# Transposing x by the DMA engine as 16-bit halves, with a new order of the first loads, in an attention and FP4 block on one core

## The chip, the cores and the metric

The kernel runs on one core of a Trainium2 chip. The core has five instruction engines that run side by side and meet at semaphores: TensorE (PE, with its weight loads listed as PEld), VectorE (DVE), ScalarE (ACT), GpSimd (POOL) and SyncE (SP), which here only issues DMAs. Sixteen DMA engines move the data. The metric is the device time of one execution in microseconds (us); lower is better.

## The reference, cut to what matters

The input is x of 16 batches, each 512 rows of 256 numbers in float32. All arithmetic is float32 unless said otherwise.

```
q, k, v = x Wq + bq, x Wk + bk, x Wv + bv          # 16 heads of 16 numbers
q, k    = softmax over the 16 numbers of a head     # p / (sum p + 1e-6)
ctx     = (q k^T / (sum q + 1e-6)) v                # linear attention: q (k^T v)
x1      = layernorm(x + ctx Wo + bo)
fp4(t)  = blocks of 16 along the last axis, rounded to a 4-bit grid, times the block's scale
g, u    = fp4(x1) fp4(w_gate)^T, fp4(x1) fp4(w_up)^T        # 704 numbers each
out     = layernorm(x1 + fp4(silu(g) * u) fp4(w_down)^T)
```

## The kernel before, in words

Work is cut into batches (16, called b) and into pairs (32, called i): a pair is 256 rows, two row tiles of 128, so a batch holds two pairs. The first half of the kernel, the attention, goes by batches; the second, the feed-forward part, goes by pairs.

For one batch, `load_x` brings the 512 rows into a tile `x` by a DMA that SP issues. `project` handles one pair. It calls `transposed` (line 617), which has TensorE turn four blocks of 128 by 128 of x into PSUM by multiplying with an identity matrix; ScalarE copies the result to `xT` (line 620). TensorE then multiplies `xT` by the weights of q and k (line 724, 512 columns at a time) and of v (line 734, 256 columns). A float32 multiplication is two instructions in the profile, a transpose is one. VectorE adds the biases as it empties the banks (lines 727 and 740) and finds the largest value of each head (line 746), GpSimd subtracts it (line 750). `features` takes the exponential on ScalarE for a whole batch (line 761), sums it on VectorE (763 to 774) and scales it on GpSimd (line 780). `key_values` forms k^T v and multiplies it with Wo (lines 793 and 807). `attend` transposes q on TensorE (again `transposed`), multiplies (line 835) and calls `norm`. GpSimd has prepared x plus the bias of Wo as `xb` (line 828), and that is the last use of the tile `x`. The finished x1 goes to DRAM from ACT's DMA queue and comes back later (line 853) into one of `X1` buffers.

`norm` is a layer norm in five steps on three engines: VectorE adds and sums (line 678), ScalarE forms the negative mean and the squares (685, 687), GpSimd takes the reciprocal root with a power (691 to 693), ScalarE writes the result (700). For the very last pair it is called once for each of its two row tiles.

For one pair, `quantise` rounds x1 to FP4 codes, which a DMA transposes as 16-bit numbers from SBUF to SBUF (line 864, tile `xcT`); the scales are transposed by TensorE, written to DRAM and read back spread out (line 666), and GpSimd multiplies both (line 869). `gate_up` is 64 matmul instructions of 352 columns (line 889), a SiLU on ScalarE (894), a product on VectorE (896), and the rounding of the result in `codes` (lines 635 to 648). The codes go through a transposing DMA of 128 by 1408 (line 928, tile `hcT`). `down` multiplies with w_down (line 946), adds x1 in `norm` and writes the output. The weights are themselves rounded to FP4 inside the kernel, by `weight_scales` and `fp4_exact`, a long run of VectorE, GpSimd and ScalarE instructions (lines 477 to 548), before the first `gate_up` can start.

The order of all this is not that of the source. Every step is recorded in a `Plan` with an engine, a cost in us, a due time, and what it reads and writes. `Plan.order` simulates the engines and, among the steps that can start, takes the earliest and at a tie the one with the least due time. The result is a fixed order on each engine; at run time each engine follows its own order and waits at semaphores. Each tag of a tile has a fixed number of buffers, and a step that needs a new one waits until the oldest is free. Eight banks of PSUM are used: seven are shared by the transposes, the gate and up products and all other products. `LEAD = 9` sets the due times of attention so that it runs about nine batches ahead of the feed-forward part; `PAIR = 25.0` is the due-time step of a pair.

The first loads stand outside the plan, in `load_all` (lines 425 to 444). SP issues x of batch 0 and the three biases; ACT issues Wq, Wk, Wv, then the large gate and up weights, then w_down; SP issues the tails of gate and up. Both are in-order queues, so ScalarE's first copy stands behind its six DMAs. Wo and its bias follow x of batch 1 on SP (`load_wo`).

## Time and profile before

Three runs gave 818.48, 820.97 and 820.93 us, a median of 820.93.

| | |
|---|---|
| profiled execution, its own time | 821.11 us |
| its span in the profile | 818.9 us |
| PE busy | 786.8 us, 96% |
| DVE busy | 611.6 us, 75% |
| ACT busy | 412.3 us, 50% |
| POOL busy | 417.7 us, 51% |
| transposes of x on PE (line 617, from x) | 128 instructions |
| transposing DMAs (lines 864 and 928) | 32 and 31 |

The span is divided on the page into 40 slices of about 20.5 us; one digit stands for the busy tenths of an engine in a slice. The chain is the work that ended last, followed back from the last instruction to what released it at each step. Busy time alone says little here, because the attention, the rounding of the weights and the feed-forward part load the engines differently; it is read by stretches of time.

### The profile page before, as it was taken

What the parts mean: (1) busy time and instruction counts of PE and PEld (TensorE: products, weight loads), DVE (VectorE), ACT (ScalarE), POOL (GpSimd) and SP (SyncE); (2) the same over time, 40 slices, a digit from 0 to 9 for tenths busy, and PEclk for the clock granted to TensorE, in tenths of its full rate; (3) what the DMA queues carried; (4) which work ended last, traced back from release to release, by engine and by line L of the source; (5) the groups of instructions that cost most, each with busy time, mean ns of one, the idle gap of its engine ahead of it and who ended that gap; (6) DMA issues with size and microseconds to landing.
All of it is one profiled execution on the core that took longest, in us unless ns stands there. A gap on an engine that the chain in (4) does not pass through costs nothing.

```text
span 818.9 us, 10331 instructions
## 1 busy us (share of the span) xinstructions
PE 786.8 (96%) x3246; PEld 568.3 (69%) x3246; DVE 611.6 (75%) x1200; ACT 412.3 (50%) x924; POOL 417.7 (51%) x513
## 2 busy tenths in 40 slices
PE   5889998999999999999999999999999999999996
PEld 3566676767776767777777677777767777677674
DVE  1998998998888888668766765767767677675562
ACT  1245665745776563536563654544444444444433
POOL 0478786869888564536463534333333324333331
PEclk9989998999999999999999999999999999999999
DMA  8102241303012437766646564779797797886431
GB/s 280 32 0 93 89 146 31 109 2 104 27 38 79 88 65 150 124 100 107 112 102 100 106 123 115 127 147 144 123 148 135 145 141 131 147 131 126 119 76 38
DMA packets 104683, 85.98 MB, mean 105 GB/s; under 512 B 65037, under 2 KB 88117, under 8 KB 104629
## 3 DMA queue, kind: packets, MB, share of 16 engines
q1 hardware_dynamic: 84680, 63.81, 42.5%
q10 hardware_dynamic: 19949, 21.52, 9.4%
q8 instruction: 25, 0.41, 0.2%
q14 instruction: 29, 0.24, 0.1%
HBM read 51.25 MB, written 18.70 MB: 85 GB/s over the span
## 4 chain that ended last, share of the span: by engine, by line
PE 85%; DVE 8%; DMA 2%; POOL 2%; ACT 2%; issue 1%; SPq 0%; ACTq 0%; POOLq 0%; DVEq 0%
PE bank L889 36%; PE bank L946 20%; PE bank L724 11%; PE bank L835 6%; PE bank L734 5%; PE bank L793 3%; PE bank L617 2%; PE bank L807 2%; POOL qk L780 1%; DMA x<-dx 1%; DMA b_qkv<-in_L_attn_bk_dram 1%; DVE mx L746 1%; PE bank L657 1%; DVE qk L727 1%; DVE fs L763 1%
## 5 line engine op out<-in xcount | busy, mean ns | idle before, releaser
L889 PE MATMUL bank<-w_guT,xqT 128*128 128x352 f32 x1024 | 310.3, 459 | 0.0
L889 PEld LDWEIGHTS bank<-w_guT,xqT 128*128 128x128 f32 x1024 | 194.2, 190 | 101.4 <-issue 0.7
L946 PE MATMUL bank<-w_dT,hq 128*128 128x256 f32 x768 | 174.8, 380 | 0.6 <-DVE r L678 0.6
L932 POOL TENSOR_TENSOR hq<-hcT,hq 128x768 f32<-128x768 bf16 (+1 forms) x62 | 94.1, 1539 | 136.5 <-DMA hq<-d_h 117.3
L946 PEld LDWEIGHTS bank<-w_dT,hq 128*128 128x128 f32 x768 | 142.1, 190 | 24.9 <-issue 3.9
L896 DVE TENSOR_TENSOR h<-bank,g 128x352 f32<-128x352 f32 x128 | 66.3, 521 | 94.6 <-PE bank L889 53.9
L724 PE MATMUL bank<-w_qkv,xT 128*128 128x512 f32 x256 | 120.6, 606 | 4.5 <-ACT xT L620 4.5
L894 ACT ACTIVATE g<-bank 128x352 f32<-128x352 f32 x128 | 58.6, 460 | 122.3 <-PE bank L889 120.3
L750 POOL TENSOR_TENSOR qk<-qk,mx 128x512 f32<-128x512 f32 x64 | 70.4, 1119 | 33.2 <-DVE mx L746 33.2
L724 PEld LDWEIGHTS bank<-w_qkv,xT 128*128 128x128 f32 x256 | 48.5, 195 | 48.6 <-issue 39.2
L780 POOL TENSOR_TENSOR qk<-qk,fr 128x512 f32<-128x512 f32 x64 | 66.6, 1067 | 26.4 <-DVE fr L774 26.4
L646 ACT ACTIVATE sq<-h,magic 128x704 f32<-128x704 uint16 x64 | 56.4, 882 | 38.5 <-DVE h L643 37.6
L734 PE MATMUL bank<-w_qkv,xT 128*128 128x256 f32 x256 | 61.8, 385 | 0.0
L691 POOL TENSOR_SCALAR var_d<-var_d 128x2 f32<-128x2 f32 (+1 forms) x33 | 6.3, 191 | 108.1 <-ACT y L687 107.9
L727 DVE TENSOR_TENSOR qk<-bank,b_qkv 128x512 f32<-128x512 f32 x64 | 42.8, 682 | 24.9 <-PE bank L724 24.8
L835 PE MATMUL bank<-M,qT 128*128 128x256 f32 x256 | 59.6, 380 | 1.0 <-ACT xT L620 0.7
L734 PEld LDWEIGHTS bank<-w_qkv,xT 128*128 128x128 f32 x256 | 48.7, 194 | 14.5 <-issue 6.9
L635 DVE TENSOR_REDUCE bank<-h 128x44 f32<-128x704 f32 x64 | 57.2, 894 | 2.0
L643 DVE SCALAR_TENSOR_TENSOR h<-h,bank 128x704 f32<-128x704 f32 x64 | 56.7, 886 | 2.0
L835 PEld LDWEIGHTS bank<-M,qT 128*128 128x128 f32 x256 | 48.2, 190 | 13.1 <-issue 4.1
L648 DVE TENSOR_SCALAR hc<-sq 128x704 uint16<-128x704 uint16 x64 | 40.8, 640 | 16.2 <-ACT sq L646 16.1
L828 POOL TENSOR_TENSOR xb<-x,b_o 128x512 f32<-128x512 f32 x32 | 42.0, 1315 | 18.9 <-DVE r L678 15.4
(128 smaller groups left out, 1075.3 us busy)
## 6 DMA issues: line engine op xcount, KB each, us to landing
hq<-d_h SPq DMA_DIRECT2D x31, 704.0 KB
x<-_attn_hidden_states_dram SPq DMA_DIRECT2D x16, 512.0 KB
dx<-x1n ACTq DMA_DIRECT2D x32, 256.0 KB
x<-dx SPq DMA_DIRECT2D x32, 256.0 KB
xs<-d_x SPq DMA_DIRECT2D x32, 256.0 KB
out_dram<-y ACTq DMA_DIRECT2D x31, 256.0 KB
d_h<-sT_h ACTq DMA_DIRECT2D x31, 44.0 KB
wdn<-in_L_ffn_w_down_dram ACTq DMA_DIRECT2D x1, 704.0 KB
```

Of the source, the lines that this page charges most:

```text
L635: op("DVE", t_dve(n), due, lambda: nc.vector.tensor_reduce(amax[:, g], b3(src()), AX.X, ALU.max, apply_absolute_value=True), ins=[src_b], ...
L643: op("DVE", t_dve(n), due, lambda: nc.vector.scalar_tensor_tensor(b3(xn()), b3(src()), TIE * UP / BIG, bcast(inv[:, g], BLK), ALU.mult, AL ...
L724: op("PE", t_pe(D2), due, lambda c=c, u=u, pqk=pqk: nc.tensor.matmul(pqk.tile, xT[:, 2 * u + c, :], w_qkv[:, c, :D2], start=c == 0, stop=c ...
L734: nc.tensor.matmul(pv[:, u * D : (u + 1) * D], xT[:, 2 * u + c, :], w_qkv[:, c, D2:], start=c == 0, stop=c == DC - 1,)
L750: op("POOL", t_pool(D2), due, lambda g=g: nc.gpsimd.tensor_tensor(qk3()[:, g, :], qk3()[:, g, :], bcast(mx[:, g], HD), ALU.subtract), ins= ...
L780: nc.gpsimd.tensor_tensor(f3, f3, bcast(r[:, t * 2 * H : (t + 1) * 2 * H], HD), ALU.mult)
L835: nc.tensor.matmul(pu(pa.tile)[:, u, :], qT[:, 2 * u + c, :], M[:, c, :], start=c == 0, stop=c == DC - 1,)
L889: op("PE", t_pe(F2), due + u * 0.2 * PAIR, lambda c=c, u=u, lo=lo, ps_=ps_: nc.tensor.matmul(ps_[:, :F2], xqT[:, 2 * u + c, :], w_guT[:, c ...
L894: op("ACT", t_act(F2), due, lambda g=g, pg=pg: nc.scalar.activation(g.tile, pg[:, :F2], AF.Silu), ins=[pg], outs=[g], table="silu")
L896: op("DVE", t_dve(F2), due, lambda g=g, h=h, pu_=pu_, k=k: nc.vector.tensor_tensor(h[:, k * F2 : (k + 1) * F2], pu_[:, :F2], g.tile, ALU.m ...
L932: op("POOL", t_pool((gs.stop - gs.start) * P), d, lambda gs=gs: nc.gpsimd.tensor_tensor(part(1)[:, gs, :], hcT[:, gs, :], part(0)[:, gs, : ...
L946: op("PE", t_pe(D), due, lambda f=f, g=g, u=u: nc.tensor.matmul(pu(pd.tile)[:, u, :], part(1)[:, g, :], w_dT[:, f + u * (f == NR), :], sta ...
```

## The change

x of batches 0 and 1 is still transposed on TensorE. For the 14 others (`b >= EARLY`), a new step `split_x` lets a transposing DMA read the batch straight from DRAM as 512 rows of 512 16-bit numbers, so that the low and the high half of every float32 come out as rows of their own, in the tile `xTr`. Four further DMAs on SP, from SBUF to SBUF, sort the rows of low halves and of high halves into the tile `xpl`. In `project`, ScalarE then writes the two halves into `xT` with two copies of 512 16-bit numbers each, the second of each float32's halves beside the first. The blocks in `xT` stand in another order than before (`2 * c + u` for `2 * u + c`), which the matmuls follow. The tile `x` itself is still loaded, since `xb` needs its rows, but with a due time three steps later from batch 3 on.

The first loads are put in another order: x of batch 0 comes in two halves; Wq, Wk and Wv stay on ACT's queue; the weights of gate, up and down move from ACT's queue to SP, behind x of batch 1, Wo and its bias (`load_rest`). The rounding of w_down is due one step later.

For the last pair, `norm` is done by VectorE with its mean and variance instructions; GpSimd keeps only the power.

The tile `qk` has three buffers in place of two. Other tiles have fewer buffers: `x` 3 (from 4), `x1` 6 (from 8), `x1n` 2 (from 3), `xn` and `sqx` 2 (from 3), `y` 1 (from 2), and the two tags `r1` and `r2` of two buffers each become one tag of three.

```diff
--- before.py
+++ after.py
@@ -19,6 +19,8 @@
 BLK = 16
 
 LEAD = 9
+
+EARLY = 2
 
 LAST = 1
 
@@ -312,7 +314,7 @@
 
     NFF = 6
 
-    X1 = 8
+    X1 = 6
     plan = Plan()
     op = plan.op
 
@@ -371,12 +373,22 @@
     xs = {}
 
     def load_x(b, due):
-        x = buf([TPB, D], "x", 4, f"x_{b}")
-        op("SP", 0.1, due, lambda: nc.sync.dma_start(x.tile, hidden[b].rearrange("(t p) d -> p t d", p=P)),
-           outs=[x])
-        op(f"DMA:x{b}" if b < 4 else "DMA", (6.0, 9.0, 16.0, 18.0, 3.5)[min(b, 4)], due, lambda: None, outs=[x])
+        x = buf([TPB, D], "x", 3, f"x_{b}")
+        rows = hidden[b].rearrange("(t p) d -> p t d", p=P)
+        if b:
+            op("SP", 0.1, due, lambda: nc.sync.dma_start(x.tile, rows), outs=[x])
+            op(f"DMA:x{b}" if b < 4 else "DMA", (0, 9.0, 16.0, 18.0, 3.5)[min(b, 4)], due, lambda: None, outs=[x])
+        else:
+
+            def halves():
+                for p in range(PPB):
+                    nc.sync.dma_start(x[:, 2 * p : 2 * p + 2, :], rows[:, 2 * p : 2 * p + 2, :])
+
+            op("SP", 0.1, due, halves, outs=[x])
+            for p in range(PPB):
+                op(f"DMA:x{b}{p}", 4.5 + p, due, lambda: None, outs=[(x, p)])
         if b == 1:
-            op("SP", 0.1, due, load_wo)
+            op("SP", 0.1, due, load_rest)
         xs[b] = x
 
     w_qkv = const.tile([P, DC, D3], F32, name="w_qkv")
@@ -417,16 +429,13 @@
 
     wqkv_in, wo_in = (loaded(n, t) for n, t in (("wqkv", 7.0), ("wo", 14.0)))
     NGU, NDN = NW * D // F2, DC * FF // F2
-    op("DMA:wgu", 13.0, 0.0, lambda: None, outs=[(gu_b, k) for k in range(NGU)])
-    op("DMA:wdn", 16.0, 0.0, lambda: None, outs=[(dn_b, k) for k in range(NDN)])
+    op("DMA:wgu", 16.0, 0.0, lambda: None, outs=[(gu_b, k) for k in range(NGU)])
+    op("DMA:wdn", 20.0, 0.0, lambda: None, outs=[(dn_b, k) for k in range(NDN)])
     wguT_b = [Fixed(f"wguT{i}") for i in range(2)]
     wdT_b = Fixed("wdT")
 
     def load_all():
 
-        gu_b.make()
-        dn_b.make()
-        gu_raw, dn_raw = gu_rows(), dn_rows()
         head = [o for o in plan.ops if o.eng == "SP"][:1]
         for o in head:
             for b in o.new:
@@ -436,16 +445,19 @@
         for i, (w, bias) in enumerate(((Wq, bq), (Wk, bk), (Wv, bv))):
             nc.scalar.dma_start(w_qkv[:, :, i * D : (i + 1) * D], w.rearrange("(c p) n -> p c n", p=P))
             nc.sync.dma_start(b_qkv[:, i * D : (i + 1) * D], bias.partition_broadcast(P))
+
+    def load_rest():
+        nc.sync.dma_start(w_o, Wo.rearrange("(c p) n -> p c n", p=P))
+        nc.sync.dma_start(b_o, bo.partition_broadcast(P))
+        gu_b.make()
+        dn_b.make()
+        gu_raw, dn_raw = gu_rows(), dn_rows()
         for i, w in enumerate((w_gate, w_up)):
-            nc.scalar.dma_start(
+            nc.sync.dma_start(
                 gu_raw[:, i * NR : (i + 1) * NR, :], w[: NR * P].rearrange("(c p) k -> p c k", p=P)
             )
             nc.sync.dma_start(gu_raw[i * TR : (i + 1) * TR, 2 * NR, :], w[NR * P :])
-        nc.scalar.dma_start(dn_raw, w_down.rearrange("(c p) k -> p c k", p=P))
-
-    def load_wo():
-        nc.sync.dma_start(w_o, Wo.rearrange("(c p) n -> p c n", p=P))
-        nc.sync.dma_start(b_o, bo.partition_broadcast(P))
+        nc.sync.dma_start(dn_raw, w_down.rearrange("(c p) k -> p c k", p=P))
 
     def fill():
         make_identity(nc, ident)
@@ -671,7 +683,24 @@
 
         n = len(us)
         key = None if n == 2 else us[0]
-        rs, nm, var, rstd, nb = (buf([n], t if n == 2 else t + "1", 3, f"{t}_{name}") for t in ("rs", "nm", "var", "rstd", "nb"))
+        if n == 1:
+            u = us[0]
+            rstd = buf([1], "rstd1", 2, f"rstd_{name}")
+            st, mv = buf([6], "st1", 2, f"st_{name}"), buf([2], "mv1", 2, f"mv_{name}")
+
+            def stats():
+                nc.vector.tensor_tensor(r[:, u, :], pu(pr.tile)[:, u, :], add(u), ALU.add)
+                nc.vector.bn_stats(st.tile, r[:, u, :])
+                nc.vector.bn_aggr(mv.tile, st.tile)
+                nc.vector.tensor_scalar(mv[:, 1:2], mv[:, 1:2], LN_EPS, None, ALU.add)
+
+            op("DVE", 2 * t_dve(D) + 0.1, due, stats, ins=[(pr, key)] + ins, outs=[(r, key), st, mv])
+            op("POOL", 0.7, due, lambda: nc.gpsimd.tensor_tensor(rstd.tile, mv[:, 1:2], neg_half[:, :1], ALU.pow), ins=[mv], outs=[rstd])
+            op("DVE", t_dve(D), due, lambda: nc.vector.tensor_scalar(
+                dst[:, u, :], r[:, u, :], mv[:, 0:1], rstd[:, 0:1], ALU.subtract, ALU.mult),
+               ins=[(r, key), mv, rstd], outs=[(dst, key)], port=True)
+            return
+        rs, nm, var, rstd, nb = (buf([n], t, 3, f"{t}_{name}") for t in ("rs", "nm", "var", "rstd", "nb"))
 
         def total():
             for k, u in enumerate(us):
@@ -706,23 +735,50 @@
 
     qks, vs, Ms = {}, {}, {}
 
+    planes = {}
+
+    def split_x(b, due):
+
+
+        t = buf([2 * DC, L], "xTr", 1, f"xTr_{b}", U16)
+        pl = planes[b] = buf([2, DC, L], "xpl", 1, f"xpl_{b}", U16)
+        dma(f"xt{b}", 8.0, due, lambda: nc.sync.dma_start_transpose(t.tile, hidden[b].bitcast(U16)),
+            outs=[t], issue=5.0)
+
+        def regroup():
+            for h in range(2):
+                for g in range(2):
+                    nc.sync.dma_start(pl[g * P // 2 : (g + 1) * P // 2, h, :, :], t[h:P:2, g::2, :])
+
+        dma(f"xg{b}", 4.0, due, regroup, ins=[t], outs=[pl], issue=1.8)
+
     def project(b, p, due):
 
         n = f"{b}_{p}"
         if p == 0:
-            qks[b] = buf([TPB, D2], "qk", 2, f"qk_{b}")
+            qks[b] = buf([TPB, D2], "qk", 3, f"qk_{b}")
             vs[b] = buf([TPB, D], "v", 2, f"v_{b}")
         x, qk, v = xs[b], qks[b], vs[b]
-        xT = transposed(
-            lambda: [x[:, 2 * p + u, c * P : (c + 1) * P] for u in range(2) for c in range(DC)],
-            "xT", f"xT_{n}", due, [x],
-        )
+        if b < EARLY:
+            xT = transposed(
+                lambda: [x[:, 2 * p + u, cc * P : (cc + 1) * P] for cc in range(DC) for u in range(2)],
+                "xT", f"xT_{n}", due, [x if b else (x, p)],
+            )
+        else:
+            xT, pl = buf([2 * DC, P], "xT", 2, f"xT_{n}"), planes[b]
+
+            def join():
+                for h in range(2):
+                    half = xT.tile.bitcast(U16).rearrange("p (c u) (n t) -> p c (u n) t", c=DC, t=2)[:, :, :, h]
+                    nc.scalar.copy(half, pl[:, h, :, p * 2 * P : (p + 1) * 2 * P])
+
+            op("ACT", 2 * (0.16 + 2 * D / 975.0), due, join, ins=[pl], outs=[xT], name="join")
         for u in range(2):
             t = 2 * p + u
             pqk = psum("pm", f"pqk_{n}_{u}")
             for c in range(DC):
                 op("PE", t_pe(D2), due, lambda c=c, u=u, pqk=pqk: nc.tensor.matmul(
-                    pqk.tile, xT[:, 2 * u + c, :], w_qkv[:, c, :D2], start=c == 0, stop=c == DC - 1
+                    pqk.tile, xT[:, 2 * c + u, :], w_qkv[:, c, :D2], start=c == 0, stop=c == DC - 1
                 ), ins=[xT, wqkv_in], outs=[pqk], holds=[qk])
             op("DVE", t_dve(D2), due, lambda t=t, pqk=pqk: nc.vector.tensor_tensor(
                 qk[:, t, :], pqk.tile, b_qkv[:, :D2], ALU.add), ins=[pqk], outs=[(qk, t)])
@@ -732,7 +788,7 @@
             for u in range(2):
                 for c in range(DC):
                     nc.tensor.matmul(
-                        pv[:, u * D : (u + 1) * D], xT[:, 2 * u + c, :], w_qkv[:, c, D2:],
+                        pv[:, u * D : (u + 1) * D], xT[:, 2 * c + u, :], w_qkv[:, c, D2:],
                         start=c == 0, stop=c == DC - 1,
                     )
 
@@ -837,9 +893,9 @@
                         start=c == 0, stop=c == DC - 1,
                     )
 
-        r = buf([2, D], "r1", 2, f"r1_{i}")
+        r = buf([2, D], "r", 3, f"r1_{i}")
         op("PE", 2 * DC * t_pe(D), due, mm_a, ins=[qT, M], outs=[pa], holds=[r, xb], name="attend")
-        x1 = buf([2, D], "x1n", 3, f"x1n_{i}")
+        x1 = buf([2, D], "x1n", 2, f"x1n_{i}")
         norm(pa, lambda u: xb[:, u, :], x1, f"a{i}", due, [xb], r, lambda u: x1[:, u, :])
 
         d = Buf(dr, [P, 2, D], "x1", NP, f"dx1_{i}")
@@ -856,7 +912,7 @@
         flat = lambda b: b.tile.rearrange("p u d -> p (u d)")
         am, iv = (small(n // BLK, t + "x", f"{t}_x{i}") for t in ("am", "iv"))
         scales = am, buf([n // BLK], "nsx", 2, f"ns_x{i}"), iv
-        xn, sq = (buf([2, D], "xq", 3, f"{t}_{i}") for t in ("xn", "sqx"))
+        xn, sq = (buf([2, D], "xq", 2, f"{t}_{i}") for t in ("xn", "sqx"))
         xc = buf([n], "xc", 2, f"xc_{i}", U16)
         codes((lambda: flat(x1), x1), (lambda: flat(xn), xn), (lambda: flat(sq), sq), xc, 0, n, scales, 0,
               f"x{i}", due)
@@ -939,7 +995,7 @@
         x1 = s["x1"]
         both, part = s["h"]
         pd = psum("pm", f"pd_{i}")
-        r = buf([2, D], "r2", 2, f"r2_{i}")
+        r = buf([2, D], "r", 3, f"r2_{i}")
         for u in range(2):
             for f in range(NR + 1):
                 g = NR if f == NR else f + u * (NR + 1)
@@ -947,7 +1003,7 @@
                     pu(pd.tile)[:, u, :], part(1)[:, g, :], w_dT[:, f + u * (f == NR), :],
                     start=f == 0, stop=f == NR,
                 ), ins=[(both, "mid" if f == NR else f"{u}b" if f == NR - 1 else f"{u}a"), wdT_b], outs=[(pd, u)], holds=[r], name="down")
-        y = buf([2, D], "y", 2, f"y_{i}")
+        y = buf([2, D], "y", 1, f"y_{i}")
         out2 = out[b, 2 * p * P : 2 * (p + 1) * P, :].rearrange("(u p) d -> p u d", p=P)
 
         for us in ((0,), (1,)) if i == NP - 1 else (range(2),):
@@ -964,7 +1020,9 @@
     T0 = 0.0
     for b in range(B):
         d = due_at(PPB * b)
-        load_x(b, d - 6 * PAIR)
+        load_x(b, d - (6 if b < EARLY + 1 else 3) * PAIR)
+        if b >= EARLY:
+            split_x(b, d - 6 * PAIR)
         for p in range(PPB):
             project(b, p, d + (p - 3) * PAIR)
         features(b, d - PAIR)
@@ -975,7 +1033,7 @@
     gus, gus_b, gu_iv = weight_scales(gu_flat, gu_b, NGU * F2, 0, "g", wdue)
     for k in range(NGU):
         fp4_exact(gu_flat, gu_b, gus, gus_b, gu_iv, k, "g", wdue)
-    ddue = wdue + 3 * PAIR
+    ddue = wdue + 4 * PAIR
     dns, dns_b, dn_iv = weight_scales(dn_flat, dn_b, NDN * F2, 5 * NGU * F2 // BLK, "d", ddue)
     for k in range(NDN):
         fp4_exact(dn_flat, dn_b, dns, dns_b, dn_iv, k, "d", ddue)
```

## The prediction

> **What bounds the kernel now.** I read the page first, then busy time by stretches, then the chain in order of time, then the groups that the change touches.
>
> ```profile
> PE 786.8 (96%) x3246; PEld 568.3 (69%) x3246; DVE 611.6 (75%) x1200; ACT 412.3 (50%) x924; POOL 417.7 (51%) x513
> PE   5889998999999999999999999999999999999996
> DVE  1998998998888888668766765767767677675562
> ```
>
> TensorE is nearly always busy, but in the first third VectorE is too. Busy time by stretches (the columns are the stretch, its length, then PE, PEld, DVE, ACT and POOL busy, granted clock, DMA share, GB/s):
>
> ```profile
> 40.00:60.00 20.00, 15.44 (x62) 11.60 (x63) 19.02 (x36) 8.34 (x16) 13.23 (x14) 0.83 0.00 0
> 102.00:125.00 23.00, 21.09 (x101) 15.44 (x99) 22.68 (x37) 14.54 (x31) 19.44 (x25) 1.00 0.47 149
> 149.00:173.00 24.00, 22.22 (x108) 16.22 (x106) 22.52 (x37) 13.92 (x30) 20.68 (x24) 1.00 0.23 72
> 173.00:214.00 41.00, 41.00 (x186) 30.07 (x187) 34.59 (x61) 26.37 (x56) 32.74 (x41) 1.00 0.15 52
> 260.00:510.00 250.00, 250.00 (x1041) 181.95 (x1040) 185.55 (x366) 133.62 (x287) 125.47 (x148) 1.00 0.58 109
> ```
>
> In 40 to 60, 102 to 125 and 149 to 173 us VectorE is full and PE has holes; in 173 to 214 and after 260 PE is full and the others have room. The chain, in order of time:
>
> ```profile
> 1.85 7.41 DMA b_qkv<-in_L_attn_bk_dram
> 9.26 0.02 issue
> 9.28 0.38 ACTq L444
> ...
> 9.68 1.28 ACT L620
> ...
> 10.98 0.59 ACT xT L620
> ...
> 11.62 6.52 PE bank L724 x8
> ...
> 189.19 1.31 PE bank L617 x12
> ```
>
> The first projection waits for ScalarE's copy of xT, which stands behind the sixth DMA on ACT's queue, not for x. The last line prices a transpose: 1.31/12 = 0.109 us of PE. The groups:
>
> ```profile
> L617 PE MATMUL bank<-ident,x 128*128 128x128 f32 x128 | 18.1, 282 | 5.7 <-DMA x<-_attn_hidden_states_dram 5.7
> L620 ACT COPY xT<-bank 128x512 f32<-128x512 f32 x32 | 17.7, 590 | 32.0 <-PE bank L617 31.5 <-ACT x1n L700 0.5
> L646 ACT ACTIVATE sqx<-xn,magic 128x512 f32<-128x512 uint16 x32 | 23.1, 721 | 13.0 <-DVE xn L643 7.1 <-DVE r L678 2.7 <-ACT sT_x L659 0.7
> ```
>
> (The 282 ns is pipelined, the spacing is 109.) The DMA side, a transposing DMA of the trace and the stretch in which it runs:
>
> ```profile
> 329.51 1.39 SPq L928 DMA_TRANSPOSE hcT<-hc  x1
> 330.40:332.70 2.30, 2.30 (x9) 1.49 (x8) 0.64 (x2) 1.58 (x7) 0.77 (x2) 1.00 0.97 176
> ```
>
> **Transposes of x.** 14 batches x 8 = 112 of the 128 go: 112 x 0.109 = 12.2 us of PE. By the same windows for the transposes of x alone, 12 stand in 60 to 102, 16 in 173 to 214, 8 in 225 to 260 and 24 after 260: 60 in stretches where PE is full, 6.5 us on the path. The other 52 (without batches 0 and 1) stand in stretches that VectorE fills, 5.7 us, worth between 0 and 5.7. VectorE's sum does not change, so I take half, 2.8.
>
> **First loads.** PE's first projection starts at 11.62. The transposes of x start at 5.67, once all of x_0 is in; then comes the wait shown above. In the new order ACT has three DMAs, so its table load (1.28) is over early. x_0 in halves, Wq, Wk, Wv and three biases are 1.66 MB; from 2 to 8 us the DMAs moved 220 to 263 GB/s, so all is in by about 2 + 1.66/0.24 = 9, Wq and Wk by 6 to 7. First transposes at about 4.5, copy at about 5.5, first projection at about 7.2: gain 4.4. Bounds: 2.6 (all of the 1.66 MB first) and 5.5. VectorE's first instruction (15.44, four half-speed matmuls after PE's start) moves with it. What is late next: the gate and up weights, on SP behind x_1, Wo and b_o. Up to them 4.0 MB are to come, at 220 to 365 GB/s about 14 to 17 us; VectorE wants them at about 20.6 - 4.4 = 16.2 or later, because in the changed order its eight instructions on batch 0 stand before. Then w_down, x_2, its transposing DMA and the regrouping, ready at 28 to 30; PE has batch 1 until about 31. I cost these at nothing; a miss holds VectorE and PE together, up to 3 us.
>
> **The transposing DMAs.** One now is 16 blocks of 128 by 128. The row above has 11 blocks in 1.39 us of issue and at most 2.3 us of full DMAs; scaled by 16/11, T = 5.4 us. From DRAM no row shows one; the same trace at its worst (390 to 398 us, beside other transfers: 2.48 us of issue and about 6 of traffic) gives T = 12.3. The four regrouping DMAs move 512 KB: 4 x 0.45 issue and some 2 us of traffic, R = 4. `xTr` and `xpl` have one buffer each, so T + R is a loop per batch, 9 to 16 us. From 20 to 258 us PE does 194/16 = 12.1 batches, one in 19.6 us: hidden by 3.6 us at worst. DMA share there is 0.09 to 0.47 and grows by about (3.3 + 2)/19.6 = 0.27. What is queued behind these waits: on SP each regrouping waits for the transposing DMA and for ScalarE's last join, and behind it stand loads of x, x1 and scales, needed a batch or more later. In the changed order all 14 lie before the first `hcT`, so the feed-forward part's SP queue is as before. Loads of x wait for GpSimd's `xb` (three buffers), as they do now (122 us of SP waiting for L828, off the path). On ScalarE the first join waits for x_2's regrouping at about 28 to 30, and behind it stand the copies of q, which GpSimd's scaling holds until 41 in any case. The load of x, due later, feeds `xb` alone, and w_down's rounding is wanted only by the first `down` at about 309: both 0.
>
> **ScalarE.** It loses 28 copies of 0.59 and gains 56 joins; the nearest row is the 16-bit input of 512, 0.72: +40.3 - 16.5 = 24 us. The cover is ScalarE's room (26.4 busy of 41, 14.5 of 23); without it each pair would cost 0.85. The joins do not wait for PE any more, so PE loses its waits for xT (0.7 + 0.5 us). I take 0.
>
> **Third `qk`.** PE waits for L780's scaling 5.6 us, nearly all in 37 to 43, and runs at a granted 0.50 after it. A third buffer lets batch 2 fill that, but VectorE is 95% busy there: bounds 0 and 5, I take 1.
>
> **Fewer buffers.** x1 at six still runs four pairs ahead on SP in the changed order. Pairs keep PE full at 14.87 us each with DVE at 11 (620 to 635). 0, up to +3 in 260 to 510, where the chain already touches `x<-dx` once.
>
> **End.** From PE's last matmul (812.61) to the last issue (816.14) are 3.53 us. After: an add of 0.42, statistics of 0.4 (estimate from the 0.69 of a 512-wide reduction), two small instructions of 0.2, the power of 0.55, a final 0.4, hops of 0.2: 2.4, gain 1.1. `y` with one buffer makes the last pair wait for the DMA of the pair before: bounds 0.6 and 1.6.
>
> **Sum.** 6.5 + 2.8 + 4.4 + 1.0 + 1.1 = 15.8. The profiled execution took 821.11, so 805.3; it stands 0.2 above the median of the runs.
>
> **A rule against it.** The chain gives 0.109 us for a transpose on PE, and the row of L928 at most 3.7 us for eleven blocks by DMA. The Trainium skill, page "VectorE: DVE Perf Modes", sections "The three transpose paths" and "Rules for kernel authors", has 390 ns on TensorE against 1309 ns by DMA for one bf16 block and advises TensorE where PSUM is a fit place. By it T would be 16 x 1.309 = 20.9 us (an estimate), the loop 25, some 5.3 us too long for 13 batches: about 821 + 69 - 16 = 874. The trace has eleven blocks in less than three of the page's times, so the measurement decides.
>
> **Rivals.** (1) VectorE bounds everything before the feed-forward part. For: by the mean durations of the rows, its work ahead of the first gate-up eviction grows from 234.4 to 242.6 us in the changed order. Against: it stands idle about 23 us between 15 and 260, mostly where PE is full. Then only start, the 32 transposes after 225 (3.5) and the end count: 9.0, so 812.
> (2) Slower: the transposing DMA from DRAM takes longer than T = 15.6, and the loop holds PE. At T = 20 it is 24 us, 4.4 us over for 13 batches, +57, less 16: 862; it costs more than it brings from T = 16.8.
> (3) No change in effect: the late weights and x_2 take back the start, and waits for buffers the rest: 818.5 to 823.
> (4) More: all 112 transposes count (+2.9) and the third `qk` fills the hole (+4): 798.
>
> **Chances.** Sum as above 0.55, (1) 0.18, (2) 0.12, (3) 0.05, (4) 0.10. The likeliest's own range, with its bounds (start 2.6 to 5.5, shared transposes 0 to 5.7, `qk` 0 to 5, buffers 0 to -3): 800 to 812, since not all of them fall on one side together. The range for 8 in 10 takes in (4) and (1) and most of (3): 798 to 821; (2) is left out. A measurement tells 0.3%, 2.5 us, from no change: faster is the sum, (1), (4) and little of (3), 0.84; same 0.04; slower 0.12.
>
> **What would show it.** After: 16 transposes of x at L629, PE near 775 us busy, first projection near 7 us, no PE wait on `xT` beyond the first batches, the SP loop under 19 us, last norm 2.4 us. Wrong if PE or ScalarE waits for `xpl`, if VectorE's first weight reduction moves past 20 us, or if PE stands idle for more between 60 and 260 us than the 5.8 us of now (the sum over the windows there), since that would be the transposes' time turned into holes.

## The result and the profile after

The changed kernel takes 816.55 us (median of 8 runs, 815.11 to 818.94) against 820.08 us for the kernel before beside it (8 runs, 818.48 to 821.50): a ratio of 0.9961, 95% interval 0.9949 to 0.9974. So it is faster, by 3.5 us, where 15.8 were forecast. Its profiled execution has a span of 814.4 us (818.9 before).

The page of the changed kernel, busy time:

```profile
PE 772.9 (95%) x3134; PEld 551.4 (68%) x3134; DVE 610.9 (75%) x1206; ACT 428.2 (53%) x942; POOL 418.4 (51%) x509
```

PE has 112 instructions and 14.0 us of busy time less, yet the span is only 4.5 us shorter: the rest has become idle time. Where it lies, the stretches of the prediction show, with two longer ones below (the columns are the same: stretch, length, PE, PEld, DVE, ACT, POOL, granted clock, DMA share, GB/s):

```profile
40.00:60.00 20.00, 20.00 (x86) 14.13 (x85) 18.65 (x31) 18.00 (x35) 16.25 (x20) 1.00 0.51 135
173.00:214.00 41.00, 37.73 (x160) 26.00 (x159) 38.84 (x71) 28.22 (x62) 35.10 (x43) 1.00 0.43 109
```

The holes of before at 40 to 60, 102 to 125 and 149 to 173 are nearly gone (PE is idle there for 0.0, 0.0 and 0.6 us). But 173 to 214, which was full, has 3.3 us of idle PE, and 260 to 510, which was full too, has 12.0. Longer stretches, two of the kernel before and then the same two of the changed kernel:

```profile
60.00:260.00 200.00, 194.16 (x878) 140.71 (x877) 178.47 (x323) 124.58 (x280) 162.41 (x201) 0.98 0.21 69
260.00:520.00 260.00, 258.70 (x1076) 188.47 (x1075) 192.93 (x385) 138.89 (x303) 129.43 (x154) 1.00 0.57 107
60.00:260.00 200.00, 182.49 (x794) 128.82 (x793) 179.87 (x329) 137.10 (x295) 164.87 (x202) 0.99 0.43 111
260.00:520.00 260.00, 247.96 (x1001) 178.08 (x1000) 180.64 (x370) 134.62 (x298) 119.68 (x143) 0.99 0.58 114
```

From such rows comes the account that the rest of this text goes by: PE's idle time (length less busy) in five stretches, its busy time and the granted clock of the profiled execution. The two lower rows are experiments that are explained below.

| | 0-20 | 20-60 | 60-260 | 260-520 | 520-end | idle | PE busy | clock | span |
|---|---|---|---|---|---|---|---|---|---|
| before | 9.7 | 7.2 | 5.8 | 1.3 | 8.1 | 32.1 | 786.8 | 0.990 | 818.9 |
| after | 5.0 | 0.0 | 17.5 | 12.0 | 7.0 | 41.5 | 772.9 | 0.994 | 814.4 |
| a_early8 | 4.8 | 0.2 | 15.8 | 1.3 | 7.0 | 29.1 | 773.9 | 0.991 | 803.0 |
| loads_early8 | 5.1 | 1.9 | 6.7 | 0.3 | 7.2 | 21.1 | 780.1 | 1.000 | 801.2 |

The first 60 us won 11.9 us of idle time (16.9 to 5.0), more than twice the 5.4 that the forecast had for the start and the third `qk`. From 60 to 520 us 22.4 us were lost again (7.1 to 29.5).

The chain of the changed kernel at the start, in order of time:

```profile
1.31 4.38 DMA x<-_attn_hidden_states_dram
...
5.73 1.12 PE bank L629 x4
6.85 4.89 PE bank L780 x8
```

The first projection stands at 6.85 (11.62 before; forecast 7.2). It now waits for the first half of x alone. And the chain at a place in the feed-forward part, and beside it, from the timeline, what SP and VectorE did around the piece before it (473.26 to 483.37 in the chain):

```profile
495.60 0.54 DVE h L952
...
496.15 9.63 DMA x<-dx
...
505.87 0.06 DVE bank L647
...
507.83 1.19 DVE hc L660
509.01 0.12 DVE ns_h L651
...
509.18 0.31 PE bank L669
```

```profile
470.39 1.38 SPq L984 DMA_TRANSPOSE hcT<-hc  x1
...
471.87 0.63 SPq L678 DMA_DIRECT2D hq<-d_h  x1
...
473.26 0.41 SPq L909 DMA_DIRECT2D x<-dx  x1
...
483.46 0.69 DVE L647 TENSOR_REDUCE bank<-x 128x32 f32<-128x512 f32 x1 [2.97 <-DMA x<-dx]
```

`x<-dx` is the load of x1, the input of the feed-forward part, back from DRAM (`rx1` in the plan, line 909). It is issued at 473.26, a few us behind a transposing DMA and the 704 KB load of `hq`, and what it brings is first used at 483.46, 10 us later, by VectorE, which stood waiting for the last 3 us. VectorE executes in order: behind the waiting L647 stand the scales `ns_h` of the current pair, and for those PE waits (L669). The chain has four such pieces of 8.2 to 10.1 us. The waits of VectorE for this load, in the kernel before (line 635) and in the changed one, and then those of PE in the changed one:

```profile
DVE bank L635 <- DMA x<-dx: 9.2, 4, 4.3
DVE bank L647 <- DMA x<-dx: 24.7, 9, 4.7
```

```profile
PE bank L669 <- DVE ns_h L651: 7.7, 3, 3.1
PE bank L780 <- ACT xT L773: 5.8, 5, 1.9
```

(us in all, times, the longest.) The new path itself, by groups and by line:

```profile
L773 ACT COPY xT<-xpl 128x512 uint16<-128x512 uint16 x56 | 39.0, 762 | 10.3 <-DMA xpl<-xTr 5.8 <-PE bank L790 2.4 <-ACT sT_h L671 0.9
```

```profile
L751 SPq DMA_DIRECT2D xpl<-xTr x56: 593/608/894, 23.3 to 275.5; - x56
L745 SPq DMA_TRANSPOSE xTr<-_attn_hidden_states_dram x14: 1721/2043/7783, 13.5 to 267.2; - x14
```

Of the 128 transposes of x on PE 16 are left (line 629). The joins take 0.762 us (taken as 0.72). The transposing DMAs take a median of 2.0 us of issue (1.7 to 7.8), and ScalarE waits for what they bring 5.8 us in all. The shortest time from the issue of a transposing DMA to the issue of the first regrouping DMA, which needs its data, is 4.2 us (28.88 to 33.05), and 9.8 us for the first of all: the path keeps pace.

### The profile page after: what moved, and what is told of

It is laid out like the page before. It is cut to its first block, busy times and chain, and to the rows that moved or that the text cites. A ratio compares the mean times of both kernels' runs of the same rounds, so it can differ in the third digit from the quotient of the medians.

```text
span 814.4 us, 10225 instructions
## 1 busy us (share of the span) xinstructions
PE 772.9 (95%) x3134; PEld 551.4 (68%) x3134; DVE 610.9 (75%) x1206; ACT 428.2 (53%) x942; POOL 418.4 (51%) x509
## 4 chain that ended last, share of the span: by engine, by line
PE 77%; DVE 14%; DMA 5%; issue 2%; ACT 2%; POOL 0%; SPq 0%; ACTq 0%; POOLq 0%; DVEq 0%
PE bank L945 34%; PE bank L1002 19%; PE bank L780 9%; PE bank L891 5%; DMA x<-dx 4%; PE bank L790 4%; PE bank L849 2%; DVE mx L802 2%; DVE qk L783 2%; DVE fs L819 1%; PE bank L629 1%; PE bank L863 1%; DVE wxm_g L548 1%; PE bank L669 1%; DVE r L707 1%
## 5 line engine op out<-in xcount | busy, mean ns | idle before, releaser
L720 POOL TENSOR_SCALAR var_d<-var_d 128x2 f32<-128x2 f32 x31 | 6.2, 201 | 110.4 <-ACT y L716 110.2
L647 DVE TENSOR_REDUCE bank<-h 128x44 f32<-128x704 f32 x64 | 57.3, 895 | 2.1
```

The source lines that it names most:

```text
L647: op("DVE", t_dve(n), due, lambda: nc.vector.tensor_reduce(amax[:, g], b3(src()), AX.X, ALU.max, apply_absolute_value=True), ins=[src_b], ...
```

## The experiments

Each time is a median beside runs of the kernel before on the same chip, with the ratio to that and its 95% interval. "Order made anew" means that the plan was run again with the edit; "order kept" means that the instructions of TensorE, VectorE, ScalarE and GpSimd stand exactly as they did.

### Buffers of x1: x1_8 and b_x1_6

x1_8, from the changed kernel, and then b_x1_6, from the kernel before:

```diff
-    X1 = 6
+    X1 = 8
```

```diff
-    X1 = 8
+    X1 = 6
```

> The changed kernel with eight buffers for x1 in place of six; nothing else is edited, though the planner orders anew. Theory A (the holes after 260 us come from the six x1 buffers: the load of x1 for pair i+6 may be issued only after pair i is finished, takes 8 to 10 us to land and holds VectorE): the 12.0 us of PE idle between 260 and 520 us fall under 3, the time to 806 to 809. Rival A' (the loads of x1 land late because of the DMA traffic, whatever the number of buffers): 814 to 818, the waits for x1 as before.

> The kernel before with six x1 buffers in place of eight, alone. Theory A: 8 to 11 us slower than before, 828 to 831, with PE waiting behind VectorE for x1 between 300 and 520 us. Rival A': 819 to 822.

x1_8: 813.25 us, 0.9925 (0.9901 to 0.9950), just outside of both theories' ranges. VectorE still waits 21.5 us for the load, and five pieces of it stand in the chain: eight buffers, in an order made anew, win 3.3 us only. b_x1_6: 836.96 us, 1.0208 (1.0187 to 1.0230); the waits of VectorE grow from 9.2 us in 4 to 26.9 us in 12.

So taking two buffers away, in an order made anew, costs 17.5 us in the kernel before, more than expected, and giving two back in the changed kernel gives 3. The number alone does not explain both.

### One part alone: loads_only and loads_x1_8

```diff
-EARLY = 2
+EARLY = 16
```

> The changed kernel with EARLY = 16: all of x is transposed on TensorE again, no transposing DMA of x, no joins; first loads, last norm, buffers and third qk stay. Theory B (before the feed-forward part VectorE sets the pace, so a transpose taken from PE there only leaves a hole): the DMA transposes are worth 3 to 5 us, 819 to 822. Rival B' (they are worth their PE time and something else lost it): 12 us, 827 to 830. Rival B'' (joins and DMA traffic cost what they bring): 813 to 817.

With no transposing DMA for x, and all else of the change: 810.32 us, 0.9874 (0.9848 to 0.9899), 6.2 us faster than the whole change. No theory had that. With X1 = 8 on top:

> The changed kernel with all of x transposed on TensorE (EARLY = 16) and eight x1 buffers. Theory A: another 3 us or more under the version with six, 804 to 807. If it is the order that decides, anything from 805 to 815.

813.54 us, 0.9929 (0.9911 to 0.9946): two more buffers made it 3 us slower, though VectorE's waits on the load fell from 18.8 to 9.0 us. So in an order made anew the time does not follow the one wait that the edit is about, and edits had to be tried with the order kept.

### The transposes for nothing: b_free, b_nopath, a_nopath

b_free, from the kernel before (x itself takes the place of `xT`, and the ring of `xT` is held as it was):

```diff
+        if b < 2:
+            xT = transposed(
...
+        else:
+            xT = x
+            ring = buf([4, P], "xT", 2, f"xT_{n}")
+            blk = lambda u, c: x[:, 2 * p + u, c * P : (c + 1) * P]
```

b_nopath, from the kernel before (`gone` is true for xT of batches from 2 on; the matmuls take blocks of x):

```diff
         def tr():
-            for j, s in enumerate(srcs()):
+            for j, s in enumerate(() if gone else srcs()):
...
-        op("ACT", t_act(4 * P), due, lambda: nc.scalar.copy(dst.tile, pt.tile), ins=[pt], outs=[dst])
+        op("ACT", t_act(4 * P), due, lambda: None if gone else nc.scalar.copy(dst.tile, pt.tile), ins=[pt], outs=[dst])
```

a_nopath, from the changed kernel (the matmuls take blocks of `w_qkv`):

```diff
-        dma(f"xt{b}", 8.0, due, lambda: nc.sync.dma_start_transpose(t.tile, hidden[b].bitcast(U16)),
+        dma(f"xt{b}", 8.0, due, lambda: None,
...
-        dma(f"xg{b}", 4.0, due, regroup, ins=[t], outs=[pl], issue=1.8)
+        dma(f"xg{b}", 4.0, due, lambda: None, ins=[t], outs=[pl], issue=1.8)
...
-            op("ACT", 2 * (0.16 + 2 * D / 975.0), due, join, ins=[pl], outs=[xT], name="join")
+            op("ACT", 2 * (0.16 + 2 * D / 975.0), due, lambda: None, ins=[pl], outs=[xT], name="join")
```

> The kernel before, with the transposes of x for batches 2 to 15 left out altogether: the matmuls take the untransposed blocks of x as their stationary operand, so q, k and v of these batches are not those of the reference. No DMA, no join takes their place. It is what the 112 transposes are worth if they vanish. Theory B: only those where PE is full count, 3.5 to 6.5 us, 813.5 to 816.5. Rival B': all 12.2, 807 to 809.

> The kernel before with its order kept to the letter: the planner still sees the transposes of x and their copies for batches 2 to 15, but nothing is issued for them, and the matmuls take the untransposed blocks of x, so q, k and v of these batches are not the reference's. Theory C (what the transposes are worth is hidden by the planner's new order in the earlier run that left them out): with the old order they are worth what the rows say, 6.5 us and up to 12, 808 to 814. Rival B (VectorE hides them): 816 to 818. Rival D (leaving them out costs by itself, by the clock or by waits): over 820.

> The changed kernel with its order kept: the planner still sees the transposing DMAs, the regrouping and the joins, but nothing is issued for them, and the matmuls of batches 2 to 15 take blocks of the weights as their stationary operand, so q, k and v of these batches are not the reference's. Theory C (the order that the planner makes with the new steps and buffers loses the gain, not the steps themselves): 813 to 817, PE idle as before between 60 and 260 us. Rival E (the joins on ScalarE and the DMA traffic lose it): 804 to 809.

b_free, with the order made anew: 832.60 us, 1.0159 (1.0128 to 1.0191), slower by 13 although 12 us of PE's work are gone. PE now waits for GpSimd's scaling of q and k, whose tile `qk` has two buffers:

```profile
PE bank L617 <- POOL qk L787: 16.5, 10, 5.7
```

b_nopath, with the order kept: 814.88 us, 0.9943 (0.9927 to 0.9958). Leaving the 112 transposes and their copies out altogether is worth 4.6 us: 12.1 us of busy PE go (786.8 to 774.7), and 6.6 of them come back as idle time, 4.9 between 60 and 260. That lies between theory C and rival B. a_nopath, order kept: 812.37 us, 0.9914 (0.9886 to 0.9943): without its DMAs, regrouping and joins the changed kernel is 4.2 us faster (five runs from 808.98 to 815.60, so this price is rough), and most of the holes stay (16.4 us from 60 to 260, 8.7 from 260 to 520). So the new path costs about as much as the transposes are worth in the kernel before, and it is not what makes most of the holes.

### The price of the load in the plan: after_rx9 and its controls

```diff
-        dma(f"rx1_{i}", 3.5, due - PAIR, lambda: nc.sync.dma_start(x1.tile, d.tile), ins=[d], outs=[x1])
+        dma(f"rx1_{i}", 9.0, due - PAIR, lambda: nc.sync.dma_start(x1.tile, d.tile), ins=[d], outs=[x1])
```

> The changed kernel with one number of the plan edited: the load of x1 is planned with 9.0 us in place of 3.5, near the 8 to 10 us that it takes in the chain. Theory F (the plan places VectorE's rounding of x1 right behind a load that it thinks short, and the in-order engine waits): the waits of VectorE for x1 (24.7 us) fall under 8 and the holes of PE after 260 us under 4, 806 to 810. Rival (the buffer, not the price, makes it late): 814 to 818.

803.94 us (803.77 to 804.17), 0.9810 (0.9794 to 0.9826). One number of the plan, set to what the chain shows, takes 12.6 us off the changed kernel. No piece of the load is in the chain any more, and PE's idle time from 260 to 520 falls from 12.0 to 3.5, as theory F had it, and the time is a little below its range. The same number in the kernel before, in the kernel without the transposing DMAs, and with eight buffers:

> The kernel before with one number of its plan changed, the price of the load of x1 from 3.5 to 9.0 us, and the order made anew. VectorE waited 9.2 us for these loads before. Theory F (the wrong price costs where the buffers are few; with eight there was little to lose): 815 to 820. Rival H (every order made anew wins or loses some per cent whatever is changed, and the gain of the same number in the changed kernel was such a throw): outside of 814 to 822, on either side. Rival I (the price was the fault of the plan all along, in both kernels alike): 805 to 812, as far below as in the changed kernel.

> The changed kernel with all sixteen batches transposed by TensorE and the price of the load of x1 at 9.0; compared with the changed kernel at this price (803.9) it says what the transposing DMAs bring when the order is not in the way. PE then has some 12 us more of work. The prediction's step (6.5 for stretches where PE is full plus half of the others, 9.3 together): 811 to 815. Theory J (the transposes are worth what they were worth with the order kept, 4 to 5 us): 807 to 810. Rival K (they bring nothing or cost time, as the comparison at the old price, 810.3 against 816.6, said): 798 to 804.

> The changed kernel with the price of the load of x1 at 9.0 and eight buffers of x1, the order made anew. Theory F (with the right price the load has time enough with six buffers, and two more bring nothing): 802 to 806. Rival A (the buffers cost time in any case, by the wait for the last use): 797 to 801.

before_rx9: 828.17 us, 1.0101 (1.0075 to 1.0127). The load no longer stands among VectorE's longest waits, but PE waits in the attention part:

```profile
PE bank L617 <- POOL qk L780: 10.5, 4, 5.0
```

loads_rx9: 816.68 us, 0.9961 (0.9949 to 0.9973), outside of all three ranges and 12.7 us above after_rx9; PE waits 12.7 us for xT there, and VectorE no longer for the load. x1_8_rx9: 804.83 us, 0.9817 (0.9792 to 0.9842), the same as with six buffers. The gain of after_rx9 fits the load; but the controls went up by 9.0 us (before_rx9) and 6.4 us (loads_rx9, against the 810.32 of loads_only) with the same number, so an order made anew could not settle it (the theory of throws, H, had foreseen just that for the kernel before).

### The load early, the order kept: a_early8, a_run8, a_run8b

```diff
-        for o in plan.order():
+        seq = plan.order()
+        for i, b in enumerate(x1s):
+            b.bufs = 8
...
+            if i >= 8:
+                load = [o for o in seq if o.eng == "SP" and b in o.bufs]
+                seq.remove(load[0])
+                last = max(k for k, o in enumerate(seq) if x1s[i - 8] in o.bufs)
+                seq.insert(last + 1, load[0])
+        for o in seq:
```

(a_run8b has the line with `b.bufs = 8` alone. In a_early8 the loads of pairs 6 and 7, which find a free buffer, stand 20 places earlier on SP, by lines that are left out here.)

> The changed kernel with the order of every engine exactly as it is, and only the number of buffers of x1 at run time raised from six to eight (the order is still made for six). The load of x1 for a pair then no longer waits for the last use of x1 six pairs before, but it keeps its place on SP's queue and VectorE's rounding keeps its place. Theory A' (the buffer is what the load waits for): VectorE's waits on the load, 24.7 us, fall under 10, PE's idle time from 260 to 520 falls from 12.0 to under 6, and the time is 808 to 812. Rival G (the load waits for its place on SP's queue or takes its time to land; the buffer is not what is last): the waits stay above 18, and the time is 815 to 818. Numbers between say that each has a part.

> The changed kernel with the order of TensorE, VectorE, ScalarE and GpSimd exactly as it is; x1 has eight buffers, and on SP's queue alone the load of x1 for a pair stands two pairs earlier, right behind the last use of its new buffer. So the data is there long before VectorE's rounding comes to it. Theory A' (the landing of this load is what holds VectorE, and through VectorE PE, after 260 us): VectorE's waits on it, 24.7 us, fall under 5, PE's idle time from 260 to 520 falls from 12.0 to 2 to 5, and the time is 806 to 811. Rival G' (the waits lie beside slack, and the next wait takes their place): PE's idle time there stays above 8, and the time is 813 to 817.

> As the run before last meant it: the changed kernel with every engine's order kept, SP's too, and eight buffers of x1 at run time. (In the run named a_run8 the raised number did not reach the tiles; its instructions and waits were those of the changed kernel, so it was one more measurement of that.) Theory A': the load no longer waits for the last use six pairs before, but keeps its place on SP behind waits for other work; VectorE's waits on it fall from 24.7 to 8 to 16, and the time is 810 to 815. Rival G (its place on SP's queue and its landing time are all there is): the waits stay above 20 and the time is 815 to 818.

a_run8 is void: the raised number did not reach the tiles, so it was the changed kernel once more (816.52 us). a_early8: 803.21 us, 0.9801 (0.9776 to 0.9826), 13.3 us under the changed kernel, with the four engines' order untouched; that is more than theory A' had. The waits of VectorE for the load are gone, those of PE for `ns_h` with them, and so is the hole after 260:

```profile
60.00:260.00 200.00, 184.24 (x782) 129.67 (x781) 177.32 (x326) 134.38 (x291) 162.79 (x199) 0.97 0.43 113
260.00:520.00 260.00, 258.68 (x1055) 187.78 (x1055) 196.08 (x392) 141.85 (x313) 126.99 (x149) 1.00 0.61 121
```

1.3 us of idle PE remain there, of 12.0. a_run8b, eight buffers with the load at its old place on SP: 818.44 us, 0.9985 (0.9969 to 1.0002), no gain at all, 15.2 us above a_early8 beside which it was measured, and VectorE waits as in the changed kernel:

```profile
DVE bank L647 <- DMA x<-dx: 25.1, 9, 5.1
```

SP's own waits for the last use of the old buffer, 14.1 us in the changed kernel, are gone in a_run8b; yet of the twelve loads after 300 us all but one go out within about 2 us of when they did. The load that was issued at 473.26 in the changed kernel:

```profile
472.65 0.45 SPq L911 DMA_DIRECT2D x<-dx  x1
```

This settles it: what held VectorE was when the load is issued on SP's queue and how long it takes until its data can be used. The buffers matter only as the room that an earlier place needs.

### The same repair elsewhere: b_early8 and loads_early8

The edit is that of a_early8, in the kernel before (its own eight buffers, so without the lines for pairs 6 and 7) and in loads_only (`EARLY = 16`), with their own orders kept.

> The kernel before with the order of TensorE, VectorE, ScalarE and GpSimd kept and the same repair as in a_early8: on SP's queue alone the load of x1 for a pair stands right behind the last use of its buffer (eight buffers as it had). It is the control for the repair. Theory A' (the repair is worth what the load made PE stand idle; before that was at most 1.3 us from 260 to 520): 816 to 820. Rival I (the fault was worth as much in the kernel before, so that the change has nothing to do with it): 804 to 811.

> The changed kernel with all sixteen batches transposed by TensorE (the run loads_only, 810.3 us, with VectorE's 18.8 us of waits for x1 and 4.4 us of PE's idle time from 260 to 520), and the same repair on SP's queue, the order of the four engines kept. Against a_early8 (803.2) it says what the transposing DMAs bring when the loads of x1 hold nobody. Theory J (the repair gives 2 to 4, and the transposes are worth the 4 to 5 of the runs with the order kept): 806 to 809. The prediction's step (9.3 for the transposes): 811 to 814, which asks that the repair gives nothing here. Rival K (the transposes bring nothing on the path): 800 to 805.

b_early8: 818.16 us, 0.9983 (0.9971 to 0.9995). VectorE's 9.2 us of waits for the load are gone, and 1.6 us are won: the kernel before had next to nothing of this fault on its path. loads_early8: 802.90 us, 0.9794 (0.9779 to 0.9808): the fastest of all, level with a_early8 (803.21), and with every transpose of x on TensorE. So between these two kernels, in which the loads of x1 hold nobody, the transposing DMAs bring nothing. But each has an order of its own, made for its `EARLY`, and other such pairs differ: with `EARLY = 2` the kernel is slower by 6.2 us in the first pair (816.55 to 810.32), even in the second (x1_8 813.25, loads_x1_8 813.54) and faster by 12.7 in the third (after_rx9 803.94, loads_rx9 816.68), where no load of x1 holds VectorE either. What the DMAs are worth is therefore not settled by such pairs; with the order kept, there are the 4.6 and the 4.2 us of above. The stretches of loads_early8 beside those of a_early8 show where PE's time went:

```profile
60.00:260.00 200.00, 193.32 (x902) 141.34 (x901) 180.47 (x336) 125.75 (x286) 168.72 (x205) 1.00 0.19 65
260.00:520.00 260.00, 259.71 (x1065) 187.79 (x1064) 194.67 (x390) 137.47 (x301) 123.62 (x147) 1.00 0.66 116
```

From 60 to 260 VectorE does the same in both, 336 instructions in 180.5 us here and 326 in 177.3 there; PE, relieved of its transposes, stands idle 15.8 us instead of 6.7. Busy time adds one thing more: PE's busy time, times the granted clock, is 779, 780 and 778 us in three kernels with all the transposes (before, loads_early8, loads_early8_qk2 below), so at equal work 1% of clock is about 8 us. In a_early8 it is 767, some 12 less, as the forecast had it (12.2); but at a clock of 0.991 its busy time is only 6.2 less than that of loads_early8 at 1.000, against 8.0 us more of idle time.

### VectorE relieved, the order kept: a_max8

```diff
-        op("DVE", t_dve(2 * D2), due, lambda: nc.vector.tensor_reduce(mx.tile, qk3(), AX.X, ALU.max),
+        op("DVE", t_dve(2 * D2), due, lambda: nc.vector.tensor_reduce(mx.tile, qk3()[:, :, : HD // 2], AX.X, ALU.max),
```

> The changed kernel with its order kept; VectorE takes the largest value of each head of q and k over 8 of the 16 numbers instead of all (so the softmax subtracts another number), which takes about 0.55 us from each of 32 instructions of VectorE, some 15 us of them before the feed-forward part. PE's idle time from 60 to 260 is 17.5 us and the first gate-up product starts at 256.7. Theory V (VectorE bounds the part before the feed-forward, the prediction's first rival): the first gate-up product moves to 244 to 250, and the time is 804 to 811. Rival W (the holes come from chains between engines, not from VectorE's load): the first gate-up product stays within 3 us of 256.7, and the time is 813 to 817.

813.24 us, 0.9919 (0.9900 to 0.9938). The instruction went from 1217 to 683 ns:

```profile
L802 DVE TENSOR_REDUCE mx<-qk 128x64 f32<-128x512 f32 x32 | 21.8, 683 | 0.8
```

The first gate-up product moved from 256.5 to 251.9 us and PE's idle time from 60 to 260 fell from 17.5 to 12.6, for 14 us less of VectorE (221.6 to 207.5 us busy up to that product). Its start lies between the two theories, and the time in the range of rival W: about a third of VectorE's relief reaches the end of the stretch. Its load is part of what makes these holes. Of PE's waits there in the changed kernel, 8.6 us end at an instruction of VectorE (`kvT` 3.4, `qk` 2.8, `v` 2.4), 4.4 at ScalarE's joins and 2.6 at GpSimd's scaling; what VectorE itself had waited for before these was not taken apart further.

### The third qk taken away: loads_early8_qk2

From loads_early8:

```diff
-            qks[b] = buf([TPB, D2], "qk", 3, f"qk_{b}")
+            qks[b] = buf([TPB, D2], "qk", 2, f"qk_{b}")
```

> The run loads_early8 (all transposes on TensorE, the loads of x1 early; 802.9 us) with the third buffer of qk taken away again; the order is made anew, the loads of x1 are put early as there. The kernel before had PE busy for 2.9 of the 8 us from 36 to 44, at a granted clock of 0.83; loads_early8 has it busy for all 8 at 1.00. Theory Q (the third buffer fills this hole and keeps the clock up, the prediction's 1.0 for it was far too small): the hole comes back, PE stands idle 5 to 7 us from 20 to 60 instead of 1.9, and the time is 808 to 814. Rival S (the earlier start alone shifts things so that the hole is gone; the third buffer is worth the 1.0 of the prediction): PE's idle time from 20 to 60 stays under 3.5, and the time is 801 to 806.

829.93 us, 1.0134 (1.0114 to 1.0155), 27 us slower, more than either theory said. PE's idle time is 3.9 us from 20 to 60, 15.5 from 60 to 260 and 5.4 from 260 to 520, and the clock is 0.986. The window from 36 to 44 us, where the kernel before had its hole, is full here too, though at a lower clock, and what is idle from 20 to 60 lies beside it (2.0 us from 30 to 36, 1.9 from 44 to 50). PE waits for GpSimd's scaling all through the attention part, not in one hole:

```profile
36.00:44.00 8.00, 8.00 (x36) 6.18 (x36) 7.40 (x16) 6.91 (x11) 6.01 (x7) 0.93 0.00 1
PE bank L629 <- POOL qk L836: 9.4, 7, 3.3
```

The order was made anew here, so the 27 us are not the buffer alone. But the three other kernels with two buffers of `qk` and an order made anew (b_x1_6, b_free, before_rx9) are at 828 to 837 us as well, the kernel before at 820, and the eight with three buffers and an order made for them at 803 to 817. That two buffers are dear fits all of these; how dear, no run shows with the order kept.

## Why the prediction was right and wrong

The direction was right and the time, 816.55, lies in the stated range, but only because that took in the rivals; the sum's own range ended at 812. The size was not right: 15.8 us forecast, 3.5 measured. In the two profiled executions PE's busy time fell by 14.0 us, its idle time by 4.7 up to 20 us, by 7.2 from 20 to 60 and by 1.0 after 520; it rose by 11.7 from 60 to 260 and by 10.7 from 260 to 520. The forecast had both rises at nothing, except for half of the transposes that stand beside a full VectorE, and up to 3 us for the buffers. By its own steps:

- **First loads (4.4): right.** PE's idle time up to 20 us fell by 4.7, the first projection moved by 4.77. VectorE's first instruction moved from 15.44 to 10.16, its first weight reduction from 20.63 to 19.40 us.
- **Fewer buffers (0, up to +3): the step that failed most.** The late load of x1, to which six buffers leave no room for an earlier place, cost 13.3 us (after against a_early8; 15.2 from a_run8b). The prediction looked at the order of SP, where the load stands four pairs ahead, and not at the time between its issue and VectorE's L647. The load goes out behind a transposing DMA and the load of `hq` and needs 8 to 10 us, where the plan counts with 3.5; where VectorE waits for it after 260 us, the order has L647 only 5 to 11 instructions of VectorE behind the last use (L707) that frees the old buffer. The one piece `x<-dx` in the chain of the kernel before, which the prediction named, was the sign of it: it is 9.76 us long.
- **Transposes of x (6.5 + 2.8): failed too.** With the order kept they are worth 4.6 (b_nopath), and the path that replaces them costs about 4 (a_nopath), which leaves next to nothing, as a_early8 against loads_early8 does (803.21 to 802.90); the two prices come from two kernels, and pairs with other orders differ, as said above. The work that leaves PE was counted right, 12 us. What was wrong is the rule that a transpose counts in full where PE was full before: from 60 to 260 much of PE's work turned into holes. That VectorE sets the pace there is shown in part (a third of its relief in a_max8), the rest stays open. The prediction had named exactly this as what would make it wrong, with the bound of 5.8 us; 17.5 were found.
- **Third qk (1.0, up to 5): probably far too small.** The start, the third qk, the end and the new order together, without transposing DMAs and with the loads of x1 mended, brought 15.3 us (b_early8 818.16 to loads_early8 802.90), where the forecast's three terms are 6.5. In the two profiled executions (818.0 and 801.2 us of span) PE's idle time falls by 4.3 us up to 20 us, by 5.4 from 20 to 60 and by 1.3 after 520, and its busy time by 6.3 at the same instructions, with a clock of 0.990 and then 1.000. So start and end came as forecast; what the sum lacked is the stretch from 20 to 60, where it had 1.0, and the clock, which had no term of its own. The hole that it named is there before and gone in loads_early8, and with it the low clock (kernel before, then loads_early8):

```profile
36.00:44.00 8.00, 2.86 (x17) 2.10 (x16) 7.93 (x13) 3.27 (x7) 5.52 (x6) 0.83 0.00 0
```

```profile
36.00:44.00 8.00, 8.00 (x42) 6.45 (x42) 7.96 (x11) 5.25 (x8) 6.04 (x7) 1.00 0.00 1
```

  That VectorE is full there was no reason for so low a value: VectorE stays full (7.93 and 7.96), and PE works ahead. With two buffers and the earlier start (loads_early8_qk2) 3.9 us are idle from 20 to 60, of 7.2 before and 1.9 in loads_early8, so the buffer alone did not close the hole. How the 15.3 divide between the buffer and the new order is not settled.
- **End (1.1): right.** From the end of PE's last matmul (809.15) to the start of the last issue (811.6) are 2.5 us, 3.53 before and 2.4 forecast: about 1.0.
- **Transposing DMAs hidden: right.** The rival with 862 us did not come. The 4.2 us from the issue of a transposing DMA to that of its regrouping, at the shortest, are less than the T of 5.4, and ScalarE waits 5.8 us in all, so the loop stays well under the 19.6 us of a batch. The Trainium skill, page "VectorE: DVE Perf Modes", section "The three transpose paths", has 1309 ns for a block by DMA, 21 us for the sixteen of a batch (an estimate); the trace has these 4.2. The advice in the section "Rules for kernel authors" of the same page, to transpose on TensorE where PSUM will do, costs nothing between these two kernels (802.90 with all on TensorE, 803.21 with 112 by DMA), but not through that price.
- **ScalarE (0): nearly.** PE waits 5.8 us for the joins, in five waits, probably part of the 4 us that a_nopath gives back.

Of the rivals, (1), VectorE as the bound before the feed-forward part, comes nearest to what was found from 60 to 260 (a_max8), but it did not have the loss after 260. (3), no change, had the nearest time (818.5 at its lower end) and comes near to the other half: waits took most of the gain back, though for the load's landing and not for its buffer (a_run8b), while the late weights that it also named did not come.

That a_early8 lands at 803, near to 805.3, is luck and does not save the sum: with the fault mended, two errors in it cancel, 9.3 us for transposes that show no gain between these kernels and 6.5 us for the rest that brings 15.3. With the 13.3 of the late load the account is 15.3 - 13.3 = 2.0, beside 3.5 measured.

## What to carry to other kernels

When an order is planned ahead, the price of a DMA has to be the time until its data lands beside the traffic of its place, read from the chain, and fewer buffers can take away the slack that hid a wrong price; compare the time from issue to need, not who stands how many steps ahead. A part of a change that passes through a planner is to be tried with the order kept, since an order made anew made kernels slower by 13 (b_free), 9 (before_rx9) and 6 us (loads_rx9), against what the edits meant. Work taken off the busiest engine is worth little in a stretch where other engines and the chains between them set the pace: 4.6 of 12.1 us here.

## What the runs showed of the hardware

A load of 256 KB from DRAM, issued within 5 us behind a transposing DMA and a load of 704 KB on the same queue, took 8 to 10 us from its issue to its first use (chain pieces of 8.15, 8.68, 10.11 and 9.63 us). A transposing DMA of sixteen 128 by 128 blocks of 16-bit numbers straight from DRAM took a median of 2.0 us of issue, the first of them 7.8, and its data was used 4.2 us after its issue at the soonest. At the same matmuls PE was busy for 786.4 us at a granted clock of 0.990 (b_early8), 780.1 at 1.000 (loads_early8) and 789.5 at 0.986 (loads_early8_qk2). And the granted clock went with the holes at one place, 0.83 in the 8 us in which PE was busy for 2.86 and 1.00 where it was busy for all; but from 60 to 260 us, where the changed kernel was idle for 17.5 us at 0.99 and a_early8 for 15.8 at 0.97, no such rule can be read.
